# Routing norms, transposes and logits of layers 1 to 3 made by sequence inside the stage before

## The chip, the cores and the metric

The kernel runs on one core of one Trainium2 chip. The metric is the device time of one execution in microseconds (us). All weights and the input are read from device memory and the output is written there within that time. TensorE is called PE, VectorE DVE, ScalarE ACT, GpSimd POOL and SyncE SP; PEld is PE's loading of the stationary operand. Each engine takes its instructions from a queue of its own, in order.

## The reference, cut to what matters

The input x has 4 sequences of 512 tokens with 128 features. It runs through four layers, each a feed-forward part, an attention part and the same feed-forward part again, with a layer norm in front of each and the result added to x (halved for the feed-forward parts):

```python
for ffn, attn in layers:                       # 0, 1, 2, 3
    x = x + 0.5 * ffn(layernorm(x))
    x = x + attn(layernorm(x))
    x = x + 0.5 * ffn(layernorm(x))
```

The parts that the change touches:

- Layer 1: a ternary-weight network of 128 → 512 → 512 → 512 → 128 features over every token, and an attention made of running sums over the tokens.
- Layer 2's ffn: `Sm = softmax(xn @ Wr + br)` over 8 experts; each expert takes the 256 tokens for which its probability is largest, runs them through an up and a down projection, and its results, weighted by the probability, are added at those tokens.
- Layer 2's attention: linear attention with elu + 1 over 16 heads.
- Layer 3's ffn: `xn @ Wr + br` over 8 experts; each token goes to the expert with the largest logit, through three projections.
- Layer 3's attention: softmax attention over the 512 tokens of a sequence, 16 heads of 8 features.

Layer 0 has a top-2 routed ffn and a softmax attention; nothing is changed there.

## The kernel before

x stays in on-chip memory for the whole run as one tile of 128 partitions × 4 sequences × 4 token tiles × 128 features. The program is written out stage after stage. A scheduler reorders the instructions within what data, tile buffers and given dependencies allow, and fixes one order per engine.

A *norm* of a sequence is `layer_norm` (L219): on DVE four `bn_stats` (the tile st), four `bn_aggr` (mv), 13 small operations for the inverse root (L201, the tiles ir_*), and four `tensor_scalar` that write xn. `transposed` (L245) then makes four PE transposes into one PSUM bank (ps) and one ACT copy to xT.

*Layer 1* (`l1`, L906). Four sequences in two pairs, two passes k of the ffn with the attention between them. For a pair: `first` (four rounds of six matmuls into two banks p; ACT takes silu, DVE multiplies to ha and splits it into hr and hl, parts in bf16), `hidden` twice (blocks of 12 matmuls into a bank pb or pc), and `leave` (48 matmuls into po, then ot and the x update on DVE). `leave` of a pair is called when the next pair's `first` is due; of the last pair at the very end. Side work sits in a list `pieces` of generators, and each round of `first` and `hidden` takes one step of each: the attention of a sequence, the norms of the next pair. For the last pair (k, p[0]) = (1, 2) the list gets no attention.

*Layer 2's ffn* (`l2_ffn`, L1070) begins for each sequence with norm, `transposed`, four router matmuls into one shared bank lg, and a transfer of x to the rows sum. Then one add of the bias over all 16 token tiles gives lb, and softmax follows; the rows xn with the halved probabilities go to memory as xd. A search of 15 steps finds each expert's threshold, expert tokens are gathered from xd (POOL, xg), and the results are added into rows in memory, which come back as yt and are added to x, sequence by sequence (L1271).

*Layer 2's attention* (`l2_attn`, L1274): `begin(b)` is norm and transpose, `project(b)` the three projections, `leave(b)` pkv, kvm, po2, pf and the x update. The calls alternate over the sequences.

*Layer 3's ffn* (`l3_ffn`, L1340) begins like that of layer 2 (norm, xd, transpose, lg for each sequence, then one add to lb) and goes on with `first_largest`.

*Layer 3's attention* (`l3_attn`, L1551): `enter(b)` is norm and transpose; all four are called before the loop. The loop has 64 + 17 steps. A step has smax matmuls and DVE maxima (mp) for one block, and, `LAG` later, sexp matmuls, ACT exponentials e and av matmuls. `shift` brings the maxima to the queries by way of memory (pm, mT, then the transfer queries<-mT on SP). Inside the loop the PE order is the program's (`turn_of`), except where `out_of_turn` lifts it. A sequence ends with pt, rc, o, a transpose, po3a and the x update (L1633).

The eight loads of layer 3's expert weights (we<-in_e_pack_dram, L1762) are written ahead of layer 2's ffn; the time at which they start depends on when the memory that they fill is free.

Of the kernel before, what the change touches and what calls it, by code (L numbers as in the profile page):

```python
# [8 lines left out]
F32 = mybir.dt.float32  # L9
# [73 lines left out]
def kernel(  # L83
# [135 lines left out]
    def layer_norm(pool, src, name, bufs=2, width=D, twice=False):  # L219
# [5 lines left out]
        xn = pool.tile([P, TT, width], F32, tag="xn", bufs=bufs, name=f"xn_{name}")  # L225
# [12 lines left out]
        for t in range(TT):  # L238
            nc.vector.tensor_scalar(  # L239
                xn[:, t, :D], src[t], mv[:, t, 0:1], rs[:, t : t + 1],  # L240
                op0=ALU.subtract, op1=ALU.mult,
            )
        return xn
# [662 lines left out]
    def l1(aside, then):  # L906
# [5 lines left out]
        with tc.tile_pool(name="l1f", bufs=1, reuse_waits="tile") as wk, \  # L912
# [116 lines left out]
            for k in range(2):  # L1029
                for p in ((0, 1), (2, 3)):  # L1030
                    for b in p:
                        if last:
                            leave(*last.pop(0))
                            if k + p[0] and not (k == 1 and p[0] == 2):
                                pieces.append(attention((b + 2) % 4))
                        first(k, b)
# [16 lines left out]
            for r in last:  # L1053
                leave(*r)
# [15 lines left out]
    def l2_ffn(k):  # L1070
        W = D + NE
        with tc.tile_pool(name=f"l2f{k}", bufs=1, reuse_waits="tile") as wk:
# [7 lines left out]
            xd = dram.tile([T, W], F32, tag=f"xd2{k}", name=f"xd2_{k}")  # L1080
            sums_of[k, 0] = dram.tile([T, D], F32, tag=f"s{k}0", name=f"sum_{k}_0")
            xns = []
            lg = acc_bank([P, NT, NE], f"lg2_{k}")
            for b in range(B):
                xn = layer_norm(wk, x[:, b], f"c{k}_{b}", bufs=B, width=W)
                xns.append(xn)
                xT = transposed(wk, xn[:, :, :D], f"c{k}_{b}")
                for t in range(TT):
                    matmul(
                        lg[:, b * TT + t, :], lhsT=xT[:, t * P : (t + 1) * P], rhs=take(mat, MAT, "wr2"),  # L1090
                        start=True, stop=True,
                    )
                nc.sync.dma_start(
                    out=sums_of[k, 0][b * S : (b + 1) * S, :].rearrange("(t p) d -> p t d", p=P), in_=x[:, b]
                )
            lb = tmp([P, NT, NE], "lb")
            br = take(rws, ROW, "br2").unsqueeze(1).to_broadcast([P, NT, NE])
            nc.vector.tensor_tensor(lb, lg, br, op=ALU.add)
            pr = softmax(wk, lb, NT, f"c{k}")

            for b in range(B):
                nc.gpsimd.tensor_scalar(
                    xns[b][:, :, D:], pr[:, b * TT : (b + 1) * TT, :], 0.5, None, op0=ALU.mult
                )
                nc.sync.dma_start(out=xd[b * S : (b + 1) * S, :].rearrange("(t p) d -> p t d", p=P), in_=xns[b])
# [159 lines left out]
            for b in range(B):  # L1265
# [5 lines left out]
                nc.vector.tensor_tensor(x[:, b], x[:, b], y, op=ALU.add)  # L1271


    def l2_attn():  # L1274
        with tc.tile_pool(name="l2a", bufs=2, reuse_waits="tile") as wk:

            def elu1(t, shape, name):

                mn = wk.tile(shape, F32, tag="mn", name=f"mn_{name}")
                nc.vector.tensor_scalar(mn, t, 0.0, None, op0=ALU.min)  # L1280
                nc.scalar.activation(mn, mn, AF.Exp)
                o = wk.tile(shape, F32, tag=f"elu_{name[0]}", name=f"elu_{name}")
                nc.vector.scalar_tensor_tensor(o, t, 0.0, mn, op0=ALU.max, op1=ALU.add)
                return o

            xTs, qs, ks, vs = {}, {}, {}, {}

            def begin(b):
                xn = layer_norm(wk, x[:, b], f"a2_{b}")
                xTs[b] = transposed(wk, xn, f"a2_{b}")  # L1290
                nc.gpsimd.tensor_tensor(x[:, b], x[:, b], over_tiles(take(rws, ROW, "bo2")), op=ALU.add)

            def by_tokens(b, w, row):
                ps = mm_bank([P, TT, D], f"p{w}_{b}")
                for t in range(TT):
                    matmul(ps[:, t, :], lhsT=xTs[b][:, t * P : (t + 1) * P], rhs=take(mat, MAT, w), start=True, stop=True)
                o = wk.tile([P, TT, D], F32, tag=f"o_{w}", name=f"o_{w}_{b}")
                nc.vector.tensor_tensor(o, ps, over_tiles(take(rws, ROW, row)), op=ALU.add)
                return o

            def project(b):
                ks[b] = elu1(by_tokens(b, "wk2", "bk2"), [P, TT, D], f"k{b}")
                vs[b] = by_tokens(b, "wv2", "bv2")
                pq = mm_bank([P, S], f"pq2_{b}")
                matmul(pq, lhsT=take(mat, MAT, "wq2"), rhs=xTs[b], start=True, stop=True)
                qb = wk.tile([P, S], F32, tag="qb", name=f"qb_{b}")
                nc.scalar.activation(qb, pq, AF.Identity, bias=take(pcl, PCOL, "bq2"))
                qs[b] = elu1(qb, [P, S], f"q{b}")

            def leave(b):  # L1310
                pkv = acc_bank([P, D], f"pkv_{b}")
                for t in range(TT):
                    matmul(pkv, lhsT=ks[b][:, t, :], rhs=vs[b][:, t, :], start=(t == 0), stop=(t == TT - 1))

                m = wk.tile([P, D], F32, tag="kvm", name=f"kvm_{b}")
                nc.vector.tensor_tensor(m, pkv, take(cst, CONST, "heads"), op=ALU.mult)
                po = mm_bank([P, S], f"po2_{b}")
                matmul(po, lhsT=m, rhs=qs[b], start=True, stop=True)
                oT = wk.tile([P, S], F32, tag="oT", name=f"oT_{b}")
                nc.scalar.copy(oT, po)  # L1320
                pf = acc_bank([P, TT, D], f"pf2_{b}")
                for t in range(TT):
                    matmul(pf[:, t, :], lhsT=oT[:, t * P : (t + 1) * P], rhs=take(mat, MAT, "wo2"), start=True, stop=True)
                nc.vector.tensor_tensor(x[:, b], x[:, b], pf, op=ALU.add)

            begin(0)
            begin(1)
            project(0)
            for b in range(B):
                if b + 2 < B:  # L1330
                    begin(b + 2)
                if b + 1 < B:
                    project(b + 1)
                leave(b)
# [5 lines left out]
    def l3_ffn(k):  # L1340
        with tc.tile_pool(name=f"l3f{k}", bufs=1, reuse_waits="tile") as wk:
# [9 lines left out]
            xd = dram.tile([T, D], F32, tag=f"xd{k}", name=f"xd_{k}")  # L1351
            y_d = dram.tile([T, D], F32, tag=f"y3{k}", name=f"y3_{k}")
            lg = acc_bank([P, NT, NE], f"lg3_{k}")
            for b in range(B):
                nm = f"{k}_{b}"
                xn = layer_norm(wk, x[:, b], f"d{nm}")
                nc.sync.dma_start(out=xd[b * S : (b + 1) * S, :].rearrange("(t p) d -> p t d", p=P), in_=xn)
                xT = transposed(wk, xn, f"d{nm}")
                for t in range(TT):
                    matmul(  # L1360
                        lg[:, b * TT + t, :], lhsT=xT[:, t * P : (t + 1) * P], rhs=take(mat, MAT, "wr3"),
                        start=True, stop=True,
                    )
            lb = tmp([P, NT, NE], "lb")
            br = take(rws, ROW, "br3").unsqueeze(1).to_broadcast([P, NT, NE])
            nc.vector.tensor_tensor(lb, lg, br, op=ALU.add)
# [176 lines left out]
            for b in range(B):  # L1543
# [3 lines left out]
                if k == 1:  # L1547
                    nc.sync.dma_start(out=out[b].rearrange("(t p) d -> p t d", p=P), in_=x[:, b])


    def l3_attn():  # L1551
# [3 lines left out]
        with tc.tile_pool(name="l3a", bufs=1, reuse_waits="tile") as wk:  # L1555
            vps, xTs, of_qk = [], [], {}
# [10 lines left out]

            def enter(b):
                xn = layer_norm(wk, x[:, b], f"a3_{b}")
                xTs.append(transposed(wk, xn, f"a3_{b}", bufs=B))  # L1570
# [65 lines left out]
            enter(0)  # L1636
# [5 lines left out]
            for b in range(1, B):  # L1642
                enter(b)
            later = {}
            in_turn["last"] = None

# [3 lines left out]
            for s4 in range(64 + 17):  # L1650
                for half in range(2):
# [5 lines left out]
                    i, slot = s4 // 4, 2 * (s4 % 4) + half  # L1657
                    if i < 12 and i % 4 == 1 and slot in (3, 7):
                        project(i // 4 + 1, "q" if slot == 3 else "k", nc.gpsimd)
# [26 lines left out]
            in_turn.clear()  # L1686

# [26 lines left out]
    late.enter_context(psum_of("b"))  # L1714
    with tc.tile_pool(name="l0f1", bufs=1, reuse_waits="tile") as pool:
# [20 lines left out]
    def residents():  # L1736

        nonlocal mat, bdn, cst2
# [3 lines left out]
        bdn = res2.tile([P, NE, D], F32, tag="bdn", name="bdn")  # L1742
# [17 lines left out]
    for e in range(NE):  # L1760
        t = wexp3.tile([P, N_E3], F32, tag="we3", name=f"we3_{e}")
        nc.sync.dma_start(out=t, in_=e_pack[e * P : (e + 1) * P, :])  # L1762
        we3.append(t)
    l2_ffn(0)
    l2_attn()
    l2_ffn(1)
    early.close()
    l3_ffn(0)
# [161 lines left out]
```

## Time and profile before

| what | us |
|---|---|
| median of 9 runs | 1718.91 (1713.87 to 1725.25) |
| the profiled execution: its time | 1717.02 |
| its span (first to last instruction) | 1715.2 |
| granted PE clock, mean over the span | 0.871 of full |
| layer 0 ends, about | 650 |
| layer 1: last x update ends | 903.75 |
| layer 2, first ffn: routing logits lb at | 916.99 |
| its first gather (xg) | 959.10 |
| layer 2, attention: first and last x of the stage at | 1024.66, 1066.11 |
| layer 2, second ffn: lb at | 1080.97 |
| layer 3, first ffn: first x at 1185.96, lb at | 1208.00 |
| layer 3, attention: first x at | 1320.67 |
| its last x update at 1579.31, the last ffn's lb at | 1593.70 |

The times in the table's lower part are on the scale of the span. Of each stage the profile gives windows with the busy time of every engine; a timeline gives single instructions with start, duration and, in brackets, how long the engine had been idle before and which instruction released it. Tile names are shown without numbers: lg<-mat,xT_c is a router matmul, x8 means that eight records follow each other (each of the four float32 matmuls has two).

### The profile page before, as it was taken

The page shows a single profiled execution, that of the slowest core. Times are in us where ns is not written, and L with a number is a line of the kernel's source. Part 1 is how long each engine was busy: PE and PEld are TensorE (multiplying, and loading weights), DVE is VectorE, ACT ScalarE, POOL GpSimd, SP SyncE. Part 2 cuts the span into 40 slices and gives each one's busy share as a digit, 9 for nine tenths or more (in the row PEclk, how much of TensorE's full clock was granted, in tenths as well). Part 3 has the DMA queues.
Part 4 walks back from the last instruction along what each step waited for, and adds up shares of the span by engine and source line. Part 5 has one row for each costly group of instructions (what it writes and reads, how often), then busy time and mean ns, then how long its engine had stood idle before and what let it go on. Part 6 is the DMA issues. An engine that isn't in the chain of part 4 may idle for free. (4 is left out here: it accounts for less than half of the span.)

```text
span 1715.2 us, 24764 instructions
## 1 busy us (share of the span) xinstructions
PE 1366.9 (80%) x8372; PEld 850.1 (50%) x8372; DVE 1041.4 (61%) x3220; ACT 667.0 (39%) x1409; POOL 584.1 (34%) x788
## 2 busy tenths in 40 slices
PE   3999889986879999788994547363685799998685
PEld 2899324332369954343543435243585333333585
DVE  5446788885454588988856429544312888883311
ACT  1423357754632332424320113020242277775242
POOL 1162643235115353222210351054486200100485
PEclk9999689997889999899995668586698699998698
DMA  7020412221122101001303140013354423310355
GB/s 312 19 74 26 93 36 51 48 50 41 53 96 71 36 25 44 1 1 56 142 1 88 21 79 25 27 32 81 95 190 161 88 56 73 69 32 15 95 190 184
DMA packets 99832, 123.31 MB, mean 72 GB/s; under 512 B 12607, under 2 KB 87864, under 8 KB 98169
## 3 DMA queue, kind: packets, MB, share of 16 engines
q1 hardware_dynamic: 78569, 70.89, 15.3%
q0 software_dynamic: 16480, 45.98, 9.0%
q10 hardware_dynamic: 4656, 4.86, 0.8%
q8 instruction: 66, 1.08, 0.3%
q14 instruction: 61, 0.50, 0.1%
HBM read 92.93 MB, written 28.84 MB: 71 GB/s over the span
## 5 line engine op out<-in xcount | busy, mean ns | idle before, releaser
L645 DVE TENSOR_REDUCE mp<-smax 128x1 f32<-128x512 f32 (+1 forms) x512 | 323.8, 682 | 72.7 <-PE smax L161 72.0
L683 ACT ACTIVATE e<-sexp 128x512 f32<-128x512 f32 x512 | 271.8, 599 | 123.2 <-PE sexp L161 119.1
L161 PE MATMUL sexp<-queries,keys 75*128 75x512 bf16 (+1 forms) x512 | 195.2, 393 | 29.4 <-DMA queries<-mT 17.4
L161 PE MATMUL smax<-keys,queries 72*128 72x512 bf16 x512 | 205.1, 417 | 11.5 <-DMA queries<-rows_q 5.2
L161 PEld LDWEIGHTS <-queries 72*128 72x128 bf16 x512 | 52.5, 103 | 147.6 <-issue 99.5
L479 ACT ACTIVATE gl<-pa 128x256 f32<-128x256 f32 x160 | 61.0, 384 | 159.4 <-PE pa L161 109.8
L161 PE MATMUL pa<-xTe,we 128*128 128x256 f32 (+1 forms) x528 | 121.8, 386 | 1.4 <-DVE xTe L468 1.0
L161 PEld LDWEIGHTS <-th 128*128 128x128 bf16 x768 | 74.1, 96 | 97.2 <-issue 4.4
L480 DVE TENSOR_TENSOR hid<-pa,gl 128x256 f32<-128x256 f32 x160 | 67.4, 426 | 68.5 <-ACT gl L479 68.4
L1462 POOL DMA_INDIRECT xg<-xd,src x46 | 46.8, 1017 | 179.3 <-DVE wi L1452 172.0
L161 PEld LDWEIGHTS pa<-xTe,we 128*128 128x128 f32 (+1 forms) x528 | 99.2, 192 | 16.3 <-issue 1.6
L161 PEld LDWEIGHTS po<-we,hid 128*128 128x128 f32 x768 | 90.5, 192 | 1.9
L161 PE MATMUL po<-we,hid 128*128 128x128 f32 x768 | 90.7, 275 | 0.0
L427 POOL DMA_INDIRECT slots<-xn,idx x48 | 47.2, 983 | 127.9 <-DVE idx L416 73.4
L161 PEld LDWEIGHTS <-keys 75*128 75x128 bf16 (+1 forms) x512 | 50.4, 100 | 71.6 <-DMA queries<-mT 20.9
L541 POOL DMA_INDIRECT yg<-y,idx x64 | 67.8, 1059 | 34.3 <-issue 18.8
L311 POOL MEMSET paced<- 128x256 f32 x234 | 77.2, 330 | 0.3
L161 PE MATMUL av<-e,v 128*32 128x512 f32 x512 | 73.7, 645 | 0.0
L161 PE MATMUL av<-e,vp 128*32 128x512 f32 x512 | 70.5, 619 | 0.0
L1213 POOL DMA_INDIRECT xg<-xd,idx x32 | 31.3, 978 | 89.0 <-DVE junk L1194 78.2
L164 PE MATMUL ps_a<-cst,xn_a 128*128 128x128 f32 x64 | 15.2, 360 | 57.4 <-DVE xn_a L239 57.4
L161 PE MATMUL p3b<-h3a,wd 128*128 128x128 f32 x480 | 59.3, 278 | 0.0
(425 smaller groups left out, 2917.7 us busy)
## 6 DMA issues: line engine op xcount, KB each, us to landing
we<-in_w0p_dram SPq DMA_DIRECT2D x8, 1080.0 KB
we<-in_e_pack_dram SPq DMA_DIRECT2D x8, 963.0 KB
queries<-rows SPq DMA_DIRECT2D x48, 96.0 KB
queries<-rows_q SPq DMA_DIRECT2D x48, 96.0 KB
y<-y SPq DMA_DIRECT2D x32, 128.0 KB
xs<-slots SPq DMA_DIRECT2D x24, 128.0 KB
xd<-xn_c SPq DMA_DIRECT2D x8, 272.0 KB
slots<-zero ACTq DMA_DIRECT2D x2, 1024.0 KB
```

The lines of the kernel that those rows point to most:

```text
L161: return turn_of(nc.tensor.matmul(*a, **k))
L164: return turn_of(nc.tensor.transpose(*a, **k))
L311: zeros = nc.gpsimd.memset(paced, 0.0)
L427: m = nc.gpsimd.indirect_dma_start(out=slots_of[half][:, :], out_offset=rows_in(idx[:, i, t : t + 1]), in_=xn[:, t, :], in_offset=None, bo ...
L479: nc.scalar.activation(gl, pa[:, 0], AF.Gelu_apprx_tanh)
L480: latest["ins"] = nc.vector.tensor_tensor(hids[e][:, c, :], pa[:, 1], gl, op=ALU.mult)
L541: m = nc.gpsimd.indirect_dma_start(out=yg[:, t, i], out_offset=None, in_=y_d[:, :], in_offset=rows_in(idx[:, i, t : t + 1]), bounds_check= ...
L645: return nc.vector.tensor_reduce(out=self.mp[i][:, t, j], in_=s, axis=AX.X, op=ALU.max, negate=True)
L683: return e, nc.scalar.activation(e, s, AF.Exp, scale=scale)
L1213: m = nc.gpsimd.indirect_dma_start(out=t, out_offset=None, in_=xd[:, :], in_offset=rows_at(e, h))
L1462: m = nc.gpsimd.indirect_dma_start(out=xg[i], out_offset=None, in_=xd[:, :], in_offset=rows_at(src, i), bounds_check=T - 1, oob_is_err=False,)
```

## The change

A class `Router` holds, for one ffn of layer 2 or 3, the rows xd, the tile lb and the normed sequences. Its `enter(b)` is a generator that does for one sequence what the ffn did at its start: norm, transfer (sum for layer 2, xd for layer 3), transpose, four matmuls into a bank of its own, and the bias add for that sequence's part of lb. The ffn begins with `router.lb`.

```diff
+    class Router:
...
+        def enter(self, b):
+
+            k, layer = self.k, self.layer
+            nm = f"r{layer}{k}_{b}"
+            if layer == 2:
+                xn = self.xns[b] = layer_norm(wide_rows, x[:, b], nm, bufs=B, width=D + NE, tag="xnw")
+                nc.sync.dma_start(out=self.rows(sums_of[k, 0], b), in_=x[:, b])
+            else:
+                xn = layer_norm(nxt, x[:, b], nm)
+                nc.sync.dma_start(out=self.rows(self.xd, b), in_=xn)
+            yield
+            yield
+            xT = transposed(nxt, xn[:, :, :D], nm, bufs=B)
+            yield
+            lg = acc_bank([P, TT, NE], f"lg{nm}")
+            for t in range(TT):
+                matmul(
+                    lg[:, t, :], lhsT=xT[:, t * P : (t + 1) * P], rhs=take(mat, MAT, f"wr{layer}"),
+                    start=True, stop=True,
+                )
+            br = take(rws, ROW, f"br{layer}").unsqueeze(1).to_broadcast([P, TT, NE])
+            nc.vector.tensor_tensor(self.lb[:, b * TT : (b + 1) * TT], lg, br, op=ALU.add)
+            yield
```

In layer 1 the sequences 0 and 1 are entered as side work of the last pair, 2 and 3 as each leaves:

```diff
                             leave(*last.pop(0))
-                            if k + p[0] and not (k == 1 and p[0] == 2):
+                            if (k, p[0]) == (1, 2):
+                                pieces.append(enter(b - 2))
+                            else:
                                 pieces.append(attention((b + 2) % 4))
                         first(k, b)
...
-            for r in last:
-                leave(*r)
+            for k, b in last:
+                leave(k, b)
+                run(enter(b))
```

`l2_attn` is split into `begin` and `rest`; `begin(0)` runs at the end of layer 2's first ffn, and in its sequence loop the next ffn's router takes a sequence one turn after it leaves:

```diff
+        project(0)
+        begin(1)
+        for b in range(B):
+            if b + 2 < B:
+                begin(b + 2)
+            if b + 1 < B:
+                project(b + 1)
+            leave(b)
+            if b:
+                then(b - 1)
+        then(B - 1)
```

Both ffns call `then(b)` behind each x update. In layer 3's attention sequence 0 is entered at the end of the ffn before, 1 ahead of the loop, and 2 and 3 inside it with the norm cut into pieces (`norm_in_pieces`, the same operations with yields); the last ffn's router takes the sequences 0 to 2 in the loop's tail and 3 behind it:

```diff
+            run(l3_enter(xTs, 1))
...
+            aside = [then(b) for b in range(B - 1)]
...
+                    if slot == 0 and i in (2, 6):
+                        enters.append(l3_enter(xTs, i // 4 + 2))
+                    with out_of_turn():
+                        step(aside if i >= 16 else enters)
...
+            for p in aside:
+                run(p)
+            run(then(B - 1))
```

The calls, and the two new pools of on-chip memory, `wide` for layer 2's xn rows and `nxt` for the rest (on the side of the memory where the expert weights of layer 3 lie too):

```diff
+    wide_rows = early.enter_context(tc.tile_pool(name="wide", bufs=1, reuse_waits="tile"))
...
         bdn = res2.tile([P, NE, D], F32, tag="bdn", name="bdn")
+        nxt = ctx.enter_context(tc.tile_pool(name="nxt", bufs=1, side="right", reuse_waits="tile"))
...
+    r2 = Router(0, 2)
+    l1(aside, residents, r2.enter)
...
+    begin, rest = l2_attn()
+    l2_ffn(0, r2, lambda b: begin(b) if b == 0 else None)
+    r2 = Router(1, 2)
+    rest(lambda b: run(r2.enter(b)))
+    r3 = Router(0, 3)
+    l2_ffn(1, r2, lambda b: run(r3.enter(b)))
     early.close()
+    xTs = {}
+    l3_ffn(0, r3, lambda b: run(l3_enter(xTs, b)) if b == 0 else None)
     late.close()
+    r3 = Router(1, 3)
     with psum_of("att3"):
+        l3_attn(xTs, r3.enter)
```

What is computed is the same.

## The prediction

> **What bounds the kernel now.** I read the page's busy shares first, then the slices, then windows around each boundary between stages, and at last the timelines of single engines there.
>
> ```profile
> PE 1366.9 (80%) x8372; PEld 850.1 (50%) x8372; DVE 1041.4 (61%) x3220; ACT 667.0 (39%) x1409; POOL 584.1 (34%) x788
> ...
> PE   3999889986879999788994547363685799998685
> ...
> PEclk9999689997889999899995668586698699998698
> ```
>
> No engine binds throughout. Layer 1 (about 650 to 903 us, slices 16 to 21) is PE work at 9 tenths and more; layers 2 and 3 alternate. So each boundary has to be read by itself. The windows (start:end, length, busy PE, PEld, DVE, ACT, POOL, granted clock, DMA share, GB/s):
>
> ```profile
> 800.00:815.00 15.00, 15.00 (x63) 6.50 (x62) 11.91 (x29) 7.52 (x10) 4.89 (x4) 1.00 0.43 166
> 815.00:830.00 15.00, 15.00 (x73) 7.03 (x72) 14.12 (x38) 4.23 (x7) 3.50 (x3) 1.00 0.89 360
> ...
> 845.00:860.00 15.00, 15.00 (x104) 7.93 (x102) 15.00 (x36) 5.86 (x9) 4.79 (x4) 1.00 0.06 17
> 860.00:880.00 20.00, 20.00 (x92) 8.61 (x90) 12.46 (x32) 5.14 (x8) 4.23 (x5) 1.00 0.00 1
> 880.00:900.00 20.00, 20.00 (x135) 10.40 (x133) 7.97 (x12) 4.81 (x7) 4.24 (x5) 1.00 0.01 1
> ...
> 910.00:920.00 10.00, 5.64 (x27) 4.75 (x26) 4.12 (x17) 2.76 (x4) 0.71 (x2) 0.50 0.20 51
> ```
>
> Before the first routing norm PE is never idle, and from 845 to 860 DVE isn't either: work put there lengthens the stage. After 903 the routing of layer 2 runs alone. PE's timeline there, and DVE's add that ends it:
>
> ```profile
> 905.84 1.14 PE L161 MATMUL lg<-mat,xT_c 128*128 128x8 f32 x8
> 907.96 1.88 PE L161 MATMUL lg<-mat,xT_c 128*128 128x8 f32 x8 [0.68 <-ACT xT_c L251]
> 911.52 1.88 PE L161 MATMUL lg<-mat,xT_c 128*128 128x8 f32 x8 [0.73 <-ACT xT_c L251]
> 915.07 1.88 PE L161 MATMUL lg<-mat,xT_c 128*128 128x8 f32 x8 [0.73 <-ACT xT_c L251]
> ...
> 916.99 0.29 DVE L1098 TENSOR_TENSOR lb<-lg,rws 128x128 f32<-128x128 f32 x1 [4.95 <-PE lg L161]
> ```
>
> A round is four transposes (1.09 at half clock), the copy on ACT (0.58) and eight records of lg (1.88): 3.55 us from one lg to the next, one after the other. The norms are not on this path: DVE is done 4.95 us before its add. From the end of the last x update (903.06 + 0.69) to lb: 13.2 us. The same ends L2 attention (14.2: x_3 to 1066.80, lb 1080.97), L2's second ffn (22.0 from x_0 at 1185.96 to lb 1208.00) and L3 attention:
>
> ```profile
> 1562.44 0.61 PE L161 MATMUL sexp<-queries,keys 84*128 84x512 bf16 x1 [2.36 <-DMA queries<-mT]
> 1562.98 1.94 PE L161 MATMUL av<-e,vp 128*32 128x512 f32 x8
> ...
> 1579.31 0.69 DVE L1633 TENSOR_TENSOR x<-x,po3a 128x512 f32<-128x512 f32 x1 [2.58 <-PE po3a L161]
> ...
> 1593.70 0.29 DVE L1366 TENSOR_TENSOR lb<-lg,rws 128x128 f32<-128x128 f32 x1 [5.29 <-PE lg L161]
> ```
>
> 13.7 us lie between the x update's end and lb there.
>
> **The change, part by part.** The counts of matmuls, norms and copies stay; four lb adds replace one. What decides is where they stand in each engine's queue; I read that from the instruction order of the changed program. A queue runs in order, so what stands behind a waiting instruction waits too.
>
> *A lone norm.* In a row: bn_stats 0.87, aggregates 0.37, 13 inverse-root operations at 0.20 = 2.5 where each waits for the one before, xn 1.1: 4.8 us. With ps 1.1, copy 0.6, lg 1.9, add 0.3 and some 0.5 of hand-overs, a sequence takes 9 us from x to its lb.
>
> *L1 to L2 (B1), inside layer 1.* Before, po_1 (48 matmuls, 846.2 to 848.8, 0.055 each: 2.6 us) stood between the first products of sequences 2 and 3 and kept PE busy while DVE, itself full, emptied banks; the hidden blocks began at 854.3. Now it stands behind them, and on DVE the norm of sequence 0 (its eight large operations and the small ones, 4 us) stands between the hr and hl of those products, with the add lb_0 behind lg_0. The last product needs a bank that DVE frees only behind that norm. DVE: +4.1 norm, +0.3 add, −1.4 for ot and x of sequence 1 that now come later, +1.9 for waiting until ps_0 (0.63 warm, as po's neighbours have it), copy 0.58 and lg_0 (1.04 warm, less overlap) are through; some 1.3 more in semaphores and the product's refill: the hidden blocks start 6.2 later. Sequence 1's ps and lg add 0.63 + 1.04 = 1.7 to a PE that is full, and its norm is hidden (DVE 7.97 of 20). B1 inside: **+8** (5 if the scheduler's holes are half as long, 10 if each handover costs what lb_0 does).
>
> *B1, its end.* Before, po_2 and po_3 ran back to back (896.8 to 902.3). Now po_3 stands behind ps_2 and lg_2, which wait for x_2's norm. From po_2's end, t: ot and x 1.4, norm 4.8, ps to lg 3 → t+9.2; po_3 2.64 → 11.9; ot, x 1.4; a lone norm to lb 7.6 to 8.5 → t+21.5 to t+22. Before it was 916.99 − 899.5 = t+17.5. That is +4.0 with po_3 at full clock; at half clock (lg: 1.88 against 1.04) po_3 takes 5.3, so +7. I take **+5**, between them, because the hole of about 8 us sits in front of it. Three PE rounds go (−10.6), but a second full norm chain and po_3 take their place.
>
> The trace shows the granted clock fall to 0.50 in the row from 910 after waits of 1.77 and 0.73, and av take 1.94 (1562.98) against 1.06 before PE's 0.41 and 2.36 us of waiting. [...]
>
> *The expert weights of L3.* The new pools take memory that L1's tiles held, so the eight loads (963 KB each, issued at 807 before) now stand behind sum_0, wup and wdn and wait for L1's end. SP's queue has the routed rows xd behind them. 7.7 MB at 360 GB/s take 21 us: from about 921 to 942 on the old time scale; xd needs them landed by the first gather (959.10, after DVE's search): 15 us of cover. **0**; at 166 GB/s (the window with the ramp) 46 us, and the cover would be exceeded by 8 to 12.
>
> *L2 attention (B2, B3).* Norm 0 is no longer cut up: −1.2. At the end only one round is left after x_3 (9 instead of 14.2: −5), but DVE was busy for 31 of 32 us from 1024 to 1056 (15.31 + 15.54) and gets three norms (3 × 3.8 busy = 11) less what was already interleaved; each lb_b stands in line before kvm_{b+2} or the next norm, so pkv, po2 and pf of the next sequence, and with them its x, wait for an lg. I take +9 for it. Together **+3**; −3 if only half of that shows, +7 if each of three adds waits a whole round (3.55) more.
>
> *B4.* All x arrive at 1186 together, so nothing precedes; norm 0 −1.2. PE's order is as before, but now lb_0 stands before the rest of norm 1, lb_1 before the end of norm 2, lb_2 before xn_3: DVE waits for each lg where it worked beneath it. Ends: +2.3, +1.5, +0.7 for the rounds that then wait for xn. **+3.3** (−1.5 to +4).
>
> *B5, L3's first ffn to its attention.* xn_0 comes 1.2 earlier; ps_2 and ps_3 move among the scores (0.66 each). **0** (−1.5 to +2).
>
> *B6.* Behind x_3 only sequence 3 is left: 8.8 instead of 14.4 from x_3's start: −5.6. In the loop's tail PE gets three ps (0.66) and lg (1.0 to 1.9), ACT three copies (0.58) between exponentials; one ps falls into PE's hole of 2.36. Two xd transfers stand before the late queries<-mT on SP. +3.6. **−2** (−5 to +1).
>
> That hole could be used to keep the clock up; av and sexp behind it would save (1.94 − 1.06) + 0.85, twice: −3.5, within the bound. [...]
>
> Sum: 8 + 5 + 3 + 3.3 + 0 − 2 = **+17.3**, on the profiled execution's 1717.0 (span 1715.2 and 1.8 around it): 1734.3. The median of the runs lies 1.9 above that execution, so I forecast **1736**. Adding the spreads as squares (4, 4, 5, 3, 2, 3) gives 9: 1727 to 1745 for this case alone.
>
> **Rivals.** (1) *It hides as it says.* B1 −4.2 (9 instead of 13.2), B3 −5.2, B6 −5.6, B2 −1.2: −16, 1703: faster. For it: each lb closes a wait of about 5 us on DVE, and DVE has 12 of 20 us free after 880. Against: 845 to 860 is full on both engines. It decides if norm 0's wait slips behind the last product, costing B1 under 2.
> (2) *Gains and prices cancel.* The holes inside layer 1 close and only PE's own work counts: 2 × 1.7 = 3.4; end of B1 +4, B3 −3, B4 +1.5, B6 −5.6: 0, 1719.
> (3) *Slower still.* The late weights outlast the search: +10 at 166 GB/s on top of the forecast: 1746. For it: nothing else can pass them on SP's queue. Against: 360 GB/s in the row above.
>
> **How the numbers follow.** Forecast 0.60, (1) 0.16, (2) 0.15, (3) 0.09. About 0.3% (5 us) is what a measurement tells from no change: under 1713.8 faster, above 1724.1 slower. (1) and the lower edge of (2) give faster 0.19; most of (2) and a little of the forecast's tail same 0.13; the rest 0.68. The range of 8 in 10 reaches to (2)'s lower side and to (3): 1712 to 1747.
>
> **What would show it.** po_2 to lb of L2's first ffn 21 to 25 us with a PE hole of about 8 before po_3; the first hidden block's start (854.3) 6 later; DVE waiting for PE lg three times per boundary; x_3 to lb about 9 in L3's last ffn; a first gather that still waits for DVE. I am wrong if PE stays back to back from 845 to the last po, or if gathers wait for xd.

## The result, and the profile after

The changed kernel takes 1742.11 us (median of 10 runs, 1735.78 to 1751.60), the kernel before 1719.49 (31 runs): a ratio of 1.013, 95% interval 1.0111 to 1.015, so some 22.6 us slower. The forecast was 1736, in a range of 1712 to 1747. The profiled execution took 1747.09 with a span of 1745.3; it lies 5 above its median, the one of before 2.5 below, so the two traces differ by 30 where the medians differ by 22.6.

The page's busy times and slices of the changed kernel, as shown of before:

```profile
PE 1377.9 (79%) x8372; PEld 855.9 (49%) x8372; DVE 1048.7 (60%) x3232; ACT 667.3 (38%) x1409; POOL 585.7 (34%) x788
...
PE   4999879986789997979983547453597599999586
...
PEclk9999689977899998989995667567599599999698
```

The same number of matmuls, 11 us more of busy PE: the work is the same, and some of it runs at a lower clock (0.860 over the span, before 0.871). Cutting both traces at the same instructions shows where the 30 us lie. Each number is the time from the milestone of the row above to its own, taken from the timelines:

```
to this instruction                            before  changed
ot of layer 1's fifth leave                     840.8   844.2   (code that did not change)
ot of its seventh (po_2)                         58.9    67.2   +8.3
sh of layer 2's first softmax                    18.0    23.6   +5.6
first gather xg                                  41.5    42.8   +1.3
first x update of that ffn                       65.6    65.5
first pwk of layer 2's attention                  9.5     8.7   -0.8
its first x update                               14.6    16.5   +1.9
its last x update                                17.3    31.8  +14.5
sh of the second ffn                             15.5    11.3   -4.2
first x update of that ffn                      104.4   106.1   +1.7
fle of layer 3's first ffn                       22.7    25.3   +2.6
its first x update                              112.0   111.4   -0.6
first smax of layer 3's attention                26.8    24.9   -1.9
last smax                                       202.8   205.7   +2.9
last x update                                    29.1    31.1   +2.0
fle of the last ffn                              15.0     9.2   -5.8
end of the last x update of all                 117.4   116.4   -1.0
```

The windows of the changed kernel at the places that lost most: layer 2's attention from its first to its last x update, its end, the start of layer 3's first ffn, and layer 1's end (start:end, length, busy PE, PEld, DVE, ACT, POOL, granted clock, DMA share, GB/s):

```profile
1068.40:1100.20 31.80, 25.55 (x112) 18.88 (x111) 20.90 (x95) 7.30 (x12) 0.98 (x2) 0.70 0.09 26
1100.20:1111.50 11.30, 5.99 (x24) 4.60 (x22) 5.74 (x32) 1.17 (x2) 0.00 (x0) 0.50 0.08 24
1217.60:1242.60 25.00, 12.31 (x48) 10.05 (x48) 16.16 (x108) 2.35 (x4) 0.00 (x0) 0.50 0.20 58
911.40:925.20 13.80, 7.67 (x60) 6.99 (x60) 5.84 (x29) 0.59 (x1) 0.11 (x1) 0.63 0.07 20
```

No engine is full in any of them: DVE is busy for 20.9 of 31.8 us in the attention, PE for 7.7 of 13.8 at layer 1's end. These are queues whose heads wait. Where PE is busiest, for 25.6 of the 31.8 us in the attention, its clock is at 0.70.

Inside layer 1, from the ot of the fifth leave to that of the seventh, the window of before, then of the changed kernel, and below them PE's timeline of the changed kernel at the places where it waits:

```profile
840.80:899.66 58.86, 58.86 (x340) 28.48 (x339) 39.19 (x91) 18.95 (x26) 13.26 (x13) 1.00 0.04 10
```

```profile
844.20:911.37 67.17, 62.88 (x360) 30.75 (x358) 41.91 (x101) 19.93 (x28) 13.74 (x12) 1.00 0.03 9
```

```profile
853.96 0.39 PE L161 MATMUL p<-xa,tw 128*128 128x512 bf16 x1 [1.52 <-DVE ha_a L963]
...
857.78 1.01 PE L164 MATMUL ps_r<-cst,xn_r 128*128 128x128 f32 x4 [0.89 <-DVE xn_r L239]
859.12 0.39 PE L161 MATMUL pb<-ha_a,th 128*128 128x512 bf16 x1 [0.33 <-DVE ha_a L963]
859.47 1.06 PE L161 MATMUL lgr<-mat,xT_r 128*128 128x8 f32 x8
...
871.51 0.33 PE L164 MATMUL ps_r<-cst,xn_r 128*128 128x128 f32 x1 [1.39 <-DVE xn_r L239]
```

Before, PE was never idle there. Now it waits for DVE four times (1.52, 0.89 and 0.33 for the first products and the norm of sequence 0, 1.39 for the norm of sequence 1), 4.3 us with some smaller gaps, and is busy for 4.0 us more: waits and PE's own added work each make half of the 8.3. The clock stayed at 1.00. At layer 1's end:

```profile
916.79 1.24 PE L164 MATMUL ps_r<-cst,xn_r 128*128 128x128 f32 x4 [5.46 <-DVE xn_r L239]
...
920.44 0.27 PE L161 MATMUL po<-tw,ha_c 128*128 128x128 bf16 x1
920.50 0.31 PE L161 MATMUL po<-tw,hr_c 128*128 128x128 bf16 x1
920.60 0.31 PE L161 MATMUL po<-tw,hl_c 128*128 128x128 bf16 x1
...
930.60 1.25 PE L164 MATMUL ps_r<-cst,xn_r 128*128 128x128 f32 x4 [5.46 <-DVE xn_r L239]
```

5.46 us of waiting for the norm of sequence 2 in front of po_3, whose matmuls then follow each other at 0.11 up to 924.3, and at 0.055 as before only behind that, and 5.46 again for sequence 3.

In layer 2's attention:

```profile
1079.36 0.84 PE L164 MATMUL ps_r<-cst,xn_r 128*128 128x128 f32 x3 [2.39 <-DVE xn_r L239]
1081.13 1.68 PE L161 MATMUL lgr<-mat,xT_r 128*128 128x8 f32 x8 [0.68 <-ACT xT_r L273]
1082.66 2.06 PE L161 MATMUL pkv<-o_wv,elu_k 128*128 128x128 f32 x8
...
1091.03 1.88 PE L161 MATMUL lgr<-mat,xT_r 128*128 128x8 f32 x8 [0.67 <-ACT xT_r L273]
1092.76 2.06 PE L161 MATMUL pkv<-o_wv,elu_k 128*128 128x128 f32 x8
```

Each pkv of the next sequence follows an lgr without a gap and without a wait of its own. DVE had written the last of their operands long before:

```profile
1076.90 0.68 DVE L1355 TENSOR_TENSOR o_wv<-pwv,rws 128x512 f32<-128x512 f32 x1
```

So the queue held pkv, by 5 us and more, and not its data. Before, the pkv of the next sequence followed the projection or the pf directly:

```profile
1057.06 1.05 PE L161 MATMUL pkv<-o_wv,elu_k 128*128 128x128 f32 x8
...
1061.46 1.06 PE L161 MATMUL pkv<-o_wv,elu_k 128*128 128x128 f32 x8
```

After the waits of 2.39 and 0.68 us pkv takes 2.06 instead of 1.05. The windows on both sides of that place show the granted clock at 1.00 and then at 0.50:

```profile
1076.50:1081.30 4.80, 1.73 (x8) 0.73 (x6) 4.63 (x23) 1.90 (x3) 0.00 (x0) 1.00 0.19 56
1081.50:1100.10 18.60, 16.18 (x57) 12.02 (x57) 8.34 (x45) 1.76 (x3) 0.20 (x1) 0.50 0.05 14
```

In the tail of layer 3's attention PE's hole of 2.36 us is gone; gaps of 0.7 us remain (from the last smax to the last x update; before, then changed):

```profile
1550.60:1579.30 28.70, 23.88 (x129) 7.29 (x128) 3.89 (x15) 17.96 (x36) 0.00 (x0) 0.88 0.01 2
```

```profile
1585.40:1616.00 30.60, 28.48 (x165) 12.49 (x164) 7.59 (x39) 19.36 (x38) 0.00 (x0) 0.96 0.04 11
```

PE is busy 4.6 us more in a stretch 1.9 longer, at a clock of 0.96 instead of 0.88. Behind the last x update one sequence remains:

```profile
1616.04 0.69 DVE L1682 TENSOR_TENSOR x<-x,po3a 128x512 f32<-128x512 f32 x1 [3.56 <-PE po3a L161]
...
1624.57 0.19 DVE L1131 TENSOR_TENSOR lb<-lgr,rws 128x32 f32<-128x32 f32 x1 [3.12 <-PE lgr L161]
```

8.5 us from the one to the other, where before it was 14.4. And the expert weights, on SP's queue, with the first gather:

```profile
931.39 9.38 SPq L1821 DMA_DIRECT2D we<-in_e_pack_dram  x8
942.66 13.96 SPq L1152 DMA_DIRECT2D xd<-xn_r  x4
```

```profile
977.74 1.04 POOL L1260 DMA_INDIRECT xg<-xd,idx  x1 [38.34 <-DVE junk L1241]
```

The weights do start 124 us later than before and xd stands behind them, issued by 956.6; but the first gather starts at 977.7 and waits for DVE.

### The profile page after: what moved, and what is told of

Read it like the earlier page. It is cut to its first block, busy times and chain, and to the rows that moved or that the text cites. A ratio compares the mean times of both kernels' runs of the same rounds, so it can differ in the third digit from the quotient of the medians.

```text
span 1745.3 us, 24750 instructions
## 1 busy us (share of the span) xinstructions
PE 1377.9 (79%) x8372; PEld 855.9 (49%) x8372; DVE 1048.7 (60%) x3232; ACT 667.3 (38%) x1409; POOL 585.7 (34%) x788
## 4 chain that ended last, share of the span: by engine, by line
PE 58%; DVE 19%; POOL 8%; DMA 7%; issue 5%; ACT 2%; SPq 1%; POOLq 0%; DVEq 0%; ACTq 0%
PE pa L161 9%; PE av L161 7%; PE po L161 6%; PE smax L161 6%; PE sexp L161 6%; PE pc L161 5%; PE pb L161 4%; DVE mp L667 3%; PE p3b L161 2%; POOL y L1559 2%; DMA sum<-y,idx 2%; PE lgr L161 1%; POOL paced L333 1%; PE p3a L161 1%; PE pq L161 1%
## 5 line engine op out<-in xcount | busy, mean ns | idle before, releaser
L502 DVE TENSOR_TENSOR hid<-pa,gl 128x256 f32<-128x256 f32 x160 | 67.2, 426 | 67.1 <-ACT gl L501 67.0
L1296 POOL DMA_INDIRECT sum<-y,idx x32 | 50.6, 1582 | 23.4 <-DVE y L1295 14.6
```

Of the source, the lines that this page charges most:

```text
L502: latest["ins"] = nc.vector.tensor_tensor(hids[e][:, c, :], pa[:, 1], gl, op=ALU.mult)
L1296: added[e] = nc.gpsimd.indirect_dma_start(out=sums_of[k, h][:, :], out_offset=rows_at(e, h), in_=y[:, h], in_offset=None, compute_op=ALU.add,)
```

## The experiments

The first four ran on another chip, on which the kernel before took 1737.22 us; ratios and the lengths of segments are compared, not times across chips. Of the kernel before there is no trace on that chip, and none of the changed kernel. The other runs were on two more chips, where the kernel before took 1719.91 (the fifth to the eighth) and 1717.85 us (the last).

**Layer 1 undone.** No sequence is entered beside the last pair; all four behind it.

```diff
-                            if (k, p[0]) == (1, 2):
-                                pieces.append(enter(b - 2))
-                            else:
+                            if (k, p[0]) != (1, 2):
                                 pieces.append(attention((b + 2) % 4))
...
-            for k, b in last:
-                leave(k, b)
-                run(enter(b))
+            for r in last:
+                leave(*r)
+            for b in range(B):
+                run(enter(b))
```

> Layer 1 as before the change: no sequence is entered beside the last pair's work, and all four are entered behind both of the last po. Everything else is the changed kernel, the late expert weights too. Theory (places in the queues cost the time): layer 1's inside gives back its 8.3 us and its end the 5.7 that the changed kernel's profile shows, 14 in all: 1728. Rival A (the late expert weights, or the new memory pools, cost the time): they are as late here, so 1738 or more, and the first gather waits for xd. Rival B (the added work itself costs it, wherever it stands): PE has the same work, so 1740.

Measured: 1.005 of before (1.0027 to 1.0073; 1746.32 on that chip). To po_2 58.9 us, to softmax 17.2, as before (58.9, 18.0) and 14.7 less than changed. The theory's 1728 against 1719 is a ratio of 1.005. The weights are as late here: rival A is out. Rival B is out too, since the same work was done.

**po_3 ahead of the routing.** Both leaves first, then sequences 2 and 3; 0 and 1 stay inside.

```diff
-            for k, b in last:
-                leave(k, b)
-                run(enter(b))
+            for r in last:
+                leave(*r)
+            for k, b in last:
+                run(enter(b))
```

> Only the end of layer 1 is changed: both last po are written before sequences 2 and 3 are entered; sequences 0 and 1 stay beside the last pair. Theory: the hole of PE in front of po_3 goes and only two rounds follow it, so from po_2's end to the last lb some 14 us (2.6 for po_3, 1.4 for ot and x, 4.8 + 1.7 for a norm and transposes, 3.6 for the other round) in place of 23.1: -9, 1733, and the hidden blocks stay 8 late. Rival (the chain is the norms' own length, not po_3's place): only po_3's 2.6 to 5.3 go, 1737 to 1739.

Measured: 1.012 (1.0095 to 1.0145). The segment from po_2 to softmax is 16.3 against 23.6: 7.3 go, between theory (9) and rival (2.6 to 5.3), nearer the theory; inside it stays at 67.2. The total doesn't confirm it: 1.012 against the changed kernel's 1.013, with intervals that overlap, and the theory's 1733 would be 1.008, below the interval. So the 7.3 rest on the segment alone.

Layer 2's attention is as in the changed kernel here, and PE takes its instructions there in the same order; yet its first to last x update took 27.1 us, not 31.8. The clock, half again from about 1079, came back:

```profile
1079.10:1085.70 6.60, 5.54 (x20) 4.17 (x19) 3.39 (x21) 0.59 (x1) 0.00 (x0) 0.50 0.00 0
1085.90:1094.40 8.50, 6.25 (x41) 4.68 (x40) 5.69 (x30) 1.76 (x3) 0.19 (x1) 1.00 0.11 31
```

Of the five traces with this order of PE's instructions (the changed kernel and the first, second, fourth and sixth experiment) three show 31.8 and two, this one and the sixth, 27.1 and 27.9. So some 4 of the stage's +14.5 do not come from the order alone: here they went with the clock, which was at 1.00 again after 6.6 us, where the changed kernel's stayed at 0.50 to the stage's end.

**Layer 2's attention, entered after the loop.**

```diff
             leave(b)
-            if b:
-                then(b - 1)
-        then(B - 1)
+        for b in range(B):
+            then(b)
```

> In layer 2's attention the router's sequences are entered after the whole loop over sequences, not one turn after each leaves. Theory: the 11.5 us that this stage lost come from places in the queues; they go, 1731, and the x updates stand 6 to 7 us apart again as before (48.8, 55.7, 61.7, 66.1 on the old scale). Rival (DVE, busy 31 of 32 us in the stage, has to do the norms anyway): the norms only move behind the last x, so half remains: 1736.

Measured: 1.0078 (1.0051 to 1.0105). From the first to the last x update 17.5 us, with the updates 7.0, 6.1 and 4.4 apart (before 17.3, changed 31.8); from there to softmax 14.0 (15.5 and 11.3). Together 31.5 against 43.1: 11.6 us, as the theory said.

**The logits copied by ACT.**

```diff
-            nc.vector.tensor_tensor(self.lb[:, b * TT : (b + 1) * TT], lg, br, op=ALU.add)
+            nc.scalar.copy(self.lb[:, b * TT : (b + 1) * TT], lg)
...
+            nc.vector.tensor_tensor(self.lb, self.lb, br, op=ALU.add)   # once, at the ffn's start
```

> The logits of a sequence are copied from the bank to lb by ACT, and one DVE add of the bias over all sequences follows at the ffn's start: DVE no longer waits for lg in the middle of its queue (38.6 us of waits over 16 adds in the changed kernel). Theory: in layer 2's attention PE's order is what costs (pkv of sequence 2 behind lg of sequence 0), so little goes there; at the start of layer 3's first ffn the waits of DVE are the cost (about 3 us), and 1 or 2 go in layer 1: 1737. Rival (DVE's waits in line are the main cost everywhere): some 14 us go, 1728.

Measured: 1.0127 (1.01 to 1.0155): no gain that the total shows. By segments, layer 3's first ffn goes from 25.3 to 21.8 (before 22.7), layer 1's inside from 67.2 to 66.6, and the attention of layer 2 stays at 31.8. Its third and fourth x update in this run:

```profile
1089.61 0.69 DVE L1385 TENSOR_TENSOR x<-x,pf 128x512 f32<-128x512 f32 x1 [2.99 <-PE pf L161]
1099.76 0.69 DVE L1385 TENSOR_TENSOR x<-x,pf 128x512 f32<-128x512 f32 x1 [1.85 <-PE pf L161]
```

DVE still waits for PE's pf although no lb add stands in its way: the adds cost 3.5 at one boundary and nothing between these x updates (behind the last of them the segment falls from 11.3 to 9.4).

**Layer 2's attention, norms in place, the rest after the loop.** The generator of each sequence is taken to its first yield, one turn behind each leave, and run out behind the loop.

```diff
-    rest(lambda b: run(r2.enter(b)))
+    def then2(b):
+        if b is None:
+            for p in entered:
+                run(p)
+        else:
+            entered.append(r2.enter(b))
+            next(entered[-1])
+    rest(then2)          # then2(None) is called after the loop
```

> In layer 2's attention only the norm of the router (and the transfer sum) stays one turn behind each leave; transposes, logits and the bias adds follow after the loop. The rest is the changed kernel. From the first to the last x update of that stage before took 17.3 us, the changed kernel 31.8. Theory (PE's order: pkv of the next sequence stands behind an lg that waits for a norm): 19 to 21 here, 1.006 to 1.008 of before. Rival (DVE has no room for the norms): 27 or more, 1.011 or more.

Measured: 1.0065 (1.0042 to 1.0089); 17.7 us from the first to the last x update. PE's timeline there:

```profile
1077.99 1.06 PE L161 MATMUL pkv<-o_wv,elu_k 128*128 128x128 f32 x8
...
1081.47 1.16 PE L161 MATMUL pf<-mat,oT 128*128 128x128 f32 x8 [0.73 <-ACT oT L1377]
1082.46 0.96 PE L161 MATMUL lgr<-mat,xT_r 128*128 128x8 f32 x8
```

And the window from the first to the last x update:

```profile
1065.02:1082.73 17.71, 14.93 (x94) 11.14 (x92) 17.15 (x81) 6.72 (x11) 1.02 (x2) 1.00 0.16 46
```

The lgr now follows the last pf, and pkv runs at full clock. DVE had room for the norms, though it is now busy for 17.15 of the 17.71 us (before 14.85 of 17.34), so the rival is out. The scheduler also put xn of sequence 0 behind kvm of sequence 2, so DVE's order is not quite the changed kernel's; but the norms begin in the same turns, and the 14 us are gone with PE's part moved. ACT's copies xT moved along with it; in the changed kernel ACT was busy for 7.3 of the 31.8 us there, so it was not what held the stage.

**Layer 1's side work in the later blocks.**

```diff
+                    else:
+                        pieces += [enter(0), enter(1)]      # beside the last pair's pc blocks
```

and po_3 first, as above.

> Sequences 0 and 1 are entered beside the last pair's second hidden blocks (pc), where DVE has been busy 8 of 20 us, in place of its first products; both last po stand ahead of sequences 2 and 3. The rest is the changed kernel. Theory (PE is full there, so each ps and lg costs its own 1.7): from the fifth ot to po_2's ot 62.2 us (before 58.9, the changed kernel 67.2), and 16.3 from there to softmax (before 18.0, changed 23.6): 1.006. Rival 1 (the work is hidden where DVE has room): 58.9 and 16.3, 1.004. Rival 2 (any place inside costs the same 8): 67, 1.009.

Measured: 1.0073 (1.0046 to 1.0101); 61.4 us to po_2 and 16.3 to softmax. So a sequence costs 1.25 in line there, near the theory's 1.7 and not nothing: PE was busy for 61.12 of the 61.5 us. Both segments sum to 77.7, against 76.1 with everything at the end: on a full PE the move did not pay.

**The three losing moves undone.** The edits of the first, third and fourth experiment together; layer 3's attention and the split of `begin` stay.

> All four sequences are entered behind layer 1 and behind layer 2's attention, and ACT copies the logits with one DVE add for each ffn; only layer 3's attention and the split of layer 2's begin stay as changed. By the segments of the runs so far against before: layer 1's end -0.8, start of the search +1.3, start of layer 2's attention +1.1, its end -1.3, layer 3's ffn -0.9 and its end -1.9, the score loop +2.9 and its tail +2.0, the last ffn's start -5.8: -3.4, 0.998. If the parts are not independent, or the new pools or late weights cost something of their own: 1.002 or more.

Measured: 0.9939 (0.9917 to 0.9961): 1709.58 against 1719.91, faster than both kernels, and faster than the 0.998 that was expected, which lies outside the interval. So the parts are not independent, but to the good: layer 1's end gave 3.0 instead of 0.8 and the end of layer 2's attention 4.3 instead of 1.3. PE's timeline at layer 1's end:

```profile
901.98 1.04 PE L164 MATMUL ps_r<-cst,xn_r 128*128 128x128 f32 x8
903.26 1.95 PE L161 MATMUL lgr<-mat,xT_r 128*128 128x8 f32 x16 [0.24 <-ACT xT_r L273]
906.40 1.15 PE L164 MATMUL ps_r<-cst,xn_r 128*128 128x128 f32 x4 [1.18 <-DVE xn_r L239]
908.23 1.88 PE L161 MATMUL lgr<-mat,xT_r 128*128 128x8 f32 x8 [0.68 <-ACT xT_r L273]
909.96 1.09 PE L164 MATMUL ps_r<-cst,xn_r 128*128 128x128 f32 x4
```

The norms of 0 and 1 were pulled into DVE's free time in layer 1 by the scheduler; their transposes and logits directly follow po_3, two and two, the first two still at full clock (16 records of lgr in 1.95, behind them 8 in 1.88). From po_2 to softmax 15.0 instead of 18.0. The first experiment has the same calls and the same banks there and took 17.2; what it has besides is the adds on DVE. There DVE waited for an lgr in the middle of the last norm, and PE then waited for that norm:

```profile
918.62 0.19 DVE L1130 TENSOR_TENSOR lb<-lgr,rws 128x32 f32<-128x32 f32 x1 [1.82 <-PE lgr L161]
...
919.90 1.25 PE L164 MATMUL ps_r<-cst,xn_r 128*128 128x128 f32 x4 [1.32 <-DVE xn_r L239]
```

Here the last ps follows at 909.96 without a wait. In the same way 14.0 behind the last x update of layer 2's attention (the third experiment) became 11.2. So the copies by ACT, which gave nothing in the middle of that attention, are worth 2 to 3 us at each of these ends once the work stands there.

**All sequences ahead of the score loop.**

```diff
-            run(l3_enter(xTs, 1))
+            for b in range(1, B):
+                run(l3_enter(xTs, b))
...
-                    if slot == 0 and i in (2, 6):
-                        enters.append(l3_enter(xTs, i // 4 + 2))
```

and `begin(1)` ahead of `project(0)` in layer 2's attention.

> As the run before, and in layer 3's attention all sequences are entered ahead of the loop again, and in layer 2's sequence 1 is begun ahead of the projections of 0. Theory: the loop's +2.9 is the two transposes (0.66 each) and ACT copies (0.6 each) among the scores, and goes; some 1 comes back in front of the loop; layer 2's start gives 1: -6.5 against before, 0.996. Rival (the loop's time varies by itself by that much, since its length was 203.9 to 208.0 in runs of the same loop): no gain on the run before.

Measured: 0.9953 (0.9935 to 0.997): no gain on the run before. Layer 2's start gave 1.9 (15.2 after 17.1), the loop took 203.2 instead of 205.3. In the next run the same loop took 204.9. With the sequences ahead of it the loop has been seen at 202.8, 203.2 and 204.9, with them inside at 203.9 to 208.0 (eight traces, mean 205.8). The means lie some 2 us apart, as the theory has it, but the ranges overlap; it is not settled.

**The exponential's table earlier.** The edit is to the kernel of the run before.

```diff
             xT = transposed(nxt, xn[:, :, :D], nm, bufs=B)
+            if (layer, k, b) == (2, 0, B - 1):
+                early_e = small.tile([P, 1], F32, tag="early_e", bufs=1, name="early_e")
+                nc.scalar.activation(early_e, xT[:, 0:1], AF.Exp)
```

> As the run with all sequences entered ahead of the loop, with one more ACT operation in layer 2's first router: an exponential of 128x1 behind the last copy xT, so that ACT loads its table while PE makes the last logits. Theory (the 1.3 us that every version since the change lost between softmax's subtraction and the first gather is the table load of 1.28, which before ran ahead of the wait for sh and now behind it): 41.5 again from sh_c to the first gather, against 42.8; the whole 1.3 less, about 0.994 to 0.995. Rival (another cause, the late weights' transfers for one): 42.8 stays.

Measured: 0.9935 (0.9912 to 0.9958), 1705.31 against 1717.85, and 41.5 from sh to the first gather, where the nine traces since the change all show 42.8. The total's interval overlaps that of the run before (0.9953); it is the segment that shows the gain. ACT before, in the changed kernel, and in this one:

```profile
915.04 1.28 ACT L268 ACT_TABLE_LOAD   x1
917.96 0.31 ACT L268 ACTIVATE ex_c<-sh_c 128x128 f32<-128x128 f32 x1 [1.64 <-DVE sh_c L267]
```

```profile
935.35 1.28 ACT L290 ACT_TABLE_LOAD   x1 [2.88 <-DVE sh_c L289]
936.65 0.31 ACT L290 ACTIVATE ex_c<-sh_c 128x128 f32<-128x128 f32 x1
```

```profile
916.38 1.28 ACT L1129 ACT_TABLE_LOAD   x1
917.67 0.20 ACT L1129 ACTIVATE early_e<-xT_r 128x1 f32<-128x1 f32 x1
```

The load ran behind the wait for sh in the changed kernel; before, it ran under the last logits and only the exponential waited. That is the whole 1.3. Why the load's place changed no run shows.

## Why the prediction was right, and where a step of it failed

- *Layer 1's inside, +8:* measured +8.3. DVE's order in front of the last products was the place, as the first three waits show; doing the work elsewhere (the first and sixth experiment) removes 8.3 and 5.8 of it. The two terms were off against each other: the hidden blocks get going 5.3 later, not 6.2, and sequence 1 costs 3.0 behind that, not 1.7, since its norm was not hidden: PE waits 1.39 for it.
- *Layer 1's end, +5:* +5.6. The order was the one foreseen, but +5 was a middle between two cases: most of po_3 ran at 0.11 us a matmul (the clock over it was 0.59), near the case for which the sum said +7, and it took 4.7 us instead of 5.3. PE's hole in front of it was 5.46 us up to the transposes, not about 8.
- *The late weights, 0:* right; xd was issued some 20 us ahead of the first gather. The first experiment kept them late and gave back all of layer 1's loss.
- *Layer 2's attention, +3 in all:* the step that failed. The measured sum over its rows is −0.8 + 1.9 + 14.5 − 4.2 = +11.4, above the bound of +7. (That bound doesn't follow from its own condition: three rounds of 3.55 on top of +3 would be +13.7.) The −5 behind x_3 was about right (−4.2); the term of "+9" for the stage itself measured 14.5, and its grounds were the wrong ones. The prediction put it on DVE, busy 31 of 32 us, and on the lb adds in DVE's queue. With the adds off DVE it stayed 31.8; with the transposes and logits behind the loop it fell to 17.7. PE's queue decides: pkv of sequences 2 and 3 stands behind ps and lgr of 0 and 1, which wait for a norm. PE's clock goes from 1.00 to 0.50 just behind that wait, and in the changed kernel's trace it stays there, so PE's work in the rest of the stage takes nearly twice as long (pkv 2.06 instead of 1.05); in the second experiment, where it was at 1.00 again after 6.6 us, the stage took 27.1. The forecast had pkv, po2 and pf wait for an lg, but by way of DVE's adds; PE's own order it did not price. The +1.9 in front of the first x update was not foreseen; with `begin(1)` put ahead again all but 0.6 of it goes (15.2 against 14.6 before).
- *Start of layer 3's first ffn, +3.3:* +2.6, and by the mechanism named: without the adds in line it becomes −0.9.
- *In front of layer 3's attention, 0:* −1.9, and +2.9 in the loop, which varies by about that much; +1.0 together, inside the bounds.
- *Layer 3's end, −2:* −5.8 behind x_3 as worked out, +2.0 in the tail instead of +3.6: −3.8, within the bound. The tail was 1.6 cheaper than forecast; the hole filled and the clock stayed up (0.96 instead of 0.88, and no av takes 1.94), which is what the sum left out at −3.5. Router matmuls filled the stretch along with the transposes; what transposes alone would do to the clock, no run shows.
- *Not foreseen:* the table load, +1.3.

That the sum came out near is in part luck: the missing 8 us of the attention and the better ends partly cancel, and the two profiled executions, on which the rows stand, lie 30 apart where the medians lie 22.6 apart, with some 3 of the difference in front of the fifth leave, in code that did not change. Of the rivals, "it hides as it says" holds for one place: the tail of layer 3's attention, where PE really waited. Undoing the rest gives 0.9939.

## What to carry to other kernels

In this kernel, work moved into an earlier stage was hidden only on an engine that waited there, and only where nothing of that stage stood behind it in any queue: price each engine's order by itself. PE's cost most here. The same calls in the program's text may be placed behind the stage and still start early, where the scheduler has free time on one engine. A segment between two fixed instructions can resolve 1 us where the total resolves 4 (42.8 in nine traces), but not every one does: the score loop varied by 4 us, and the attention by 4.7 at the same order of PE's instructions. Look at the clock before you read such a difference.

## What the runs showed of the hardware

- PE's clock was part of the price of a short wait here, and not a fixed part. Behind waits of 2.39 and 0.68 us in layer 2's attention the clock fell from 1.00 to 0.50 and pkv took 2.06 instead of 1.05; the window's mean clock was 0.70 where before it was 1.00. With PE's instructions in the same order the half clock lasted 6.6 us in the second experiment, whose stage took 27.1 us, and outlasted the stage in the changed kernel, where it took 31.8. Inside layer 1 waits of 1.52, 0.89 and 1.39 us left it at 1.00.
- The exponential's table load stood on either side of the wait for its operand: before, it ran ahead of that wait, under the logits; in the changed kernel behind it, 1.28 us on the path. An exponential of 128x1 placed earlier took it off again (0.20 us).
